# Loading the first layer's convolution image straight from the input, and the first weights in two parts

## The chip, the cores and the metric

The kernel runs on one core of a Trainium2 chip. The metric is the device time of one execution in microseconds (us). Engines are named as the profile names them: PE is TensorE's matmul, PEld its weight load, DVE is VectorE, ACT is ScalarE, POOL is GpSimd, and SP is SyncE, which here only issues DMA transfers. ACT and POOL issue transfers too.

## The reference, cut to what matters

Four layers, each `x = x + layer(group_norm(x))`, on an image of 4 x 32 x 32 x 16 (batch, height, width, channels). Layers 0 to 2 have this form:

```python
first = jnp.einsum('ijpq,bpqc->bijc', M2, inputs)
K = jnp.transpose(G, (2, 3, 4, 0, 1, 5)).reshape(kh, kw, c, h * w * f)
shifted = lax.conv_general_dilated(inputs, K, window_strides=(1, 1), padding='SAME', ...)
shifted = shifted.reshape(b, h, w, h, w, f)
diff = jax.nn.relu(inputs[:, :, :, None, None, :] - shifted)
second = jnp.einsum('ijpq,bpqijc->bijc', W2, diff)
return first - L * second
```

`inputs` is x after a group norm of 8 groups of two channels, with mean and variance over a batch element's whole group. The convolution is 3 x 3 with zero padding and has 16 x 1024 outputs at each of 1024 points; `second` weighs them by W, which has 1024 x 1024 values. Layer 3 is a two-dimensional filter given by a rational transfer function; the change doesn't touch its formulas.

## The kernel before

**The products of a layer.** A layer's 1024 output positions (i, j) are 128 blocks of 8. For a block and a batch element the convolution is a product of nine taps x 16 channels with 128 output columns (8 positions x 16 channels) over 1024 points. The image stands in SBUF with taps and channels on the partitions: three tiles per pair of batch elements, `ims[a]` (a is 0 for batch elements 0 and 1, 1 for 2 and 3). Tiles 0 and 1 hold four taps each, for the upper 16 and the lower 16 image rows in partitions 0 to 63 and 64 to 127; tile 2 holds the ninth tap, split into a rounded part and a remainder. So a product is six matmuls (L357): three tiles by two halves. They accumulate in a PSUM tile of 128 x 1024 (`pt`, four of them in rotation). One DVE instruction (L365) takes the minimum with zero, multiplies by W's rows and sums into `acc`.

**The jobs of `conv_layer`.** Job 0 goes through blocks 0 to 7 with batch elements 0 and 1, job 1 through the same blocks with 2 and 3; then come jobs of eight blocks with all four, and the last eight blocks are again split by pairs. After every product `step()` advances the generators in `todo`, and after every block `beside` goes one step further: `first_term` (the product with M), then, in layer 0, `impulse_response`, which prepares layer 3's filter.

**Weights.** `load_w` brings a tile of W for two blocks (1 MB: 8 rows of 8 KB, each copied to 16 partitions), always on SP's queue, from a pool of six tiles. `load_g` brings eight blocks of G: `ga` (taps of tile 0), `gb` (of tile 1), both into partitions 0 to 63 and again into 64 to 127, and `g9` (the ninth tap, copied eight times). `prepare_g` subtracts the identity's share from `ga` on POOL (L285), casts `g9` on ACT (L289) and takes the remainder on DVE (L292).

**The image of layer 0, as of later layers.** `group_norm` sums on DVE, adds across partitions by small matmuls (L103), subtracts the mean (L119) and makes `rstd` by a square root on ACT and a Newton step on DVE. `store_image` writes the normalised y in three forms into `ys[a]`, a tile with zero borders (memsets L90, L92), copies border rows into `ye[a]` on POOL and ACT, and stores both to a DRAM scratch `img[a]`. `load_image` reads the shifted images back: 24 transfers of 67.5 KB for each pair, in turn on SP, ACT and POOL (L185). In layers 1 and 2 this runs beside the products of the layer before.

**The order at the start.** The order of work is written out by hand; every engine and every queue runs its instructions in the order of the program. Before the first product: load x and the constants, load G's first eight blocks (gb on ACT's queue, the rest on SP's), norm, store both images, `prepare_g`, `load_image(0)`, the first W in two halves, the second W, `load_image(1)`, the third and the fourth W. The rest of W and G follows from within `conv_layer`.

Of the kernel before, what the change touches and what calls it, by code (L numbers as in the profile page):

```python
# [29 lines left out]
F32 = mybir.dt.float32  # L30
F32R = mybir.dt.float32r
AF = mybir.ActivationFunctionType
# [19 lines left out]


@with_exitstack
def conv_stack_kernel(ctx, tc, x, M, W, G, den, num, h0, cst, dft, one, idp, idq, out):
    nc = tc.nc

    const = ctx.enter_context(tc.tile_pool(name="const", bufs=1))
# [18 lines left out]
    ctx.enter_context(tc.manual_schedule())  # L77
    xs = xp.tile([P, B, NBLK], F32, tag="x", name="x")
    nc.sync.dma_start(out=xs, in_=x)
    cs = const.tile([P, 2 * P + C], F32, name="cs")  # L80
    nc.scalar.dma_start(out=cs, in_=cst)
    ident, avg, mid = cs[:, :P], cs[:, P : 2 * P], cs[:, 2 * P :]

# [1 line left out]
    ys, ye, img = [], [], []  # L87
    for a in range(2):
        ys.append(const.tile([P, 3, 2, 4, 34], F32, name=f"y{a}"))
        nc.gpsimd.memset(ys[a], 0.0)  # L90
        ye.append(const.tile([P, 3, 2, 4, 34], F32, name=f"e{a}"))
        nc.gpsimd.memset(ye[a], 0.0)  # L92
        img.append(dram.tile([10, C, 3, ROW], F32, name=f"img{a}"))
    hd = dram.tile([8 + C * HLEN], F32, name="hd")
    fd = dram.tile([P, B, 2, 2, S], F32, name="fd")
# [7 lines left out]
            nc.tensor.matmul(pt[:, h, : s.shape[1]], lhsT=avg[rows], rhs=s[rows], start=True, stop=True)  # L103
        return pt

    def group_norm(xt):


        nb = xt.shape[1]
        vec = lambda name: small.tile([P, B], F32, tag=name, name=name)[:, :nb]  # L110
        s = vec("s")
        nc.vector.tensor_reduce(s, xt, AX.X, ALU.add)  # L112
        yield
        pm = group_sums(s)
        mean = vec("mean")
        nc.vector.tensor_copy(mean, pm[:, 0, :nb])
        nc.vector.tensor_tensor(mean, mean, pm[:, 1, :nb], ALU.add)
        xc = work.tile([P, B, NBLK], F32, tag="xc", name="xc")[:, :nb]
        nc.vector.tensor_tensor(  # L119
            xc, xt, mean.unsqueeze(2).to_broadcast([P, nb, NBLK]), ALU.subtract  # L120
        )
        sq = junkp.tile([P, S * S], F32, tag="junk", name="sq")[:, : nb * NBLK]
        sq = sq.rearrange("p (b n) -> p b n", b=nb)
        nc.vector.tensor_tensor(sq, xc, xc, ALU.mult)
        ss = vec("ss")
        nc.vector.tensor_reduce(ss, sq, AX.X, ALU.add)
        yield
        yield
        pv = group_sums(ss)
        v = vec("v")  # L130
        nc.vector.tensor_scalar(v, pv[:, 0, :nb], 1e-5, None, ALU.add)
        nc.vector.tensor_tensor(v, v, pv[:, 1, :nb], ALU.add)

        r = vec("r")
        nc.scalar.activation(r, v, AF.Sqrt)
        ri = vec("ri")
        nc.vector.reciprocal(ri, r)
        nc.vector.tensor_tensor(ri, ri, v, ALU.mult)
        nc.vector.tensor_tensor(r, r, ri, ALU.add)
        nc.vector.tensor_scalar(r, r, 0.5, None, ALU.mult)  # L140
        rstd = vec("rstd")
        nc.vector.reciprocal(rstd, r)
        return xc, rstd.unsqueeze(2).to_broadcast([P, nb, NBLK])

    ims, yc = {}, {}

    def make_image(a, xt):

# [5 lines left out]
    def store_image(a, xc, rstd):  # L154
        split = lambda t: t.rearrange("p b (cc q) -> p b cc q", q=S)
        whole, hi, lo = (ys[a][:, k, :, :, 1:33] for k in range(3))
        y = work.tile([P, 2, NBLK], F32, tag=f"yc{a}", name=f"yc{a}")
        nc.vector.tensor_tensor(y, xc, rstd, ALU.mult)
        yc[a] = y
        nc.vector.tensor_copy(hi.bitcast(F32R), split(y))  # L160
        nc.scalar.copy(whole, split(y))
        nc.vector.tensor_tensor(lo, split(y), hi, ALU.subtract)  # L162
        nc.gpsimd.tensor_copy(ye[a][96:, :, :, 1:, :], ys[a][96:, :, :, :3, :])  # L163
        nc.scalar.copy(ye[a][:32, :, :, :3, :], ys[a][:32, :, :, 1:, :])
        flat = lambda t: t.rearrange("p k b cc x -> p (k b cc x)")
        rows = img[a].rearrange("p c k x -> p c (k x)")
        nc.sync.dma_start(out=rows[1:9].rearrange("p c x -> (p c) x"), in_=flat(ys[a]))
        nc.scalar.dma_start(out=rows[0], in_=flat(ye[a][7 * C :]))
        nc.scalar.dma_start(out=rows[9], in_=flat(ye[a][:C]))

    def load_image(a):


        ims[a] = [
            imp.tile([P, 4, 2, 4, 34], d, tag=f"im{a}{k}", name=f"im{a}{k}")
            for k, d in enumerate((F32, F32, F32R))
        ]
        taps = [(n // 4, n % 4, 0, TAPS[n]) for n in range(8)]
        taps += [(2, n, 1 + n % 2, 8) for n in range(4)]
        jobs = [(half, *tap) for tap in taps for half in range(2)]  # L180

        jobs.sort(key=lambda job: job[4] // 3 == 2 * job[0])
        for n, (half, k, slot, which, tap) in enumerate(jobs):
            at, p = 64 * half + C * slot, 4 * half + tap // 3
            (nc.sync, nc.scalar, nc.gpsimd)[n % 3].dma_start(  # L185
                out=ims[a][k][at : at + C]
                .bitcast(F32)
                .rearrange("c l b cc x -> c l (b cc x)")[:, :, :RUN],
                in_=img[a][p : p + 4, :, which, tap % 3 : tap % 3 + RUN].rearrange(
                    "l c x -> c l x"  # L190
                ),
            )
# [62 lines left out]
    def chunk(layer, ch):  # L255
        return layer + ch // (NBLK // GC), ch % (NBLK // GC)

    def load_g(layer, ch, other=None):
        layer, ch = at = chunk(layer, ch)
        if layer == 3 or at in gr:  # L260
            return
        ga = gs.tile([P, GC, P], F32, tag="ga", name="ga")
        gb = gs.tile([P, GC, P], F32, tag="gb", name="gb")
        g9 = gp.tile([P, GC, P], F32, tag="g9", name="g9")
        src = G[layer][:, bass.ts(ch, GC * P)]
        for half in range(2):
            rows = slice(64 * half, 64 * half + 64)
            nc.sync.dma_start(out=ga[rows].rearrange("r n m -> r (n m)"), in_=src[:64])
            (other or nc.sync).dma_start(out=gb[rows].rearrange("r n m -> r (n m)"), in_=src[64:P])
        nc.sync.dma_start(  # L270
            out=g9.rearrange("r n m -> r (n m)"),
            in_=src[P : P + C].unsqueeze(0).to_broadcast([8, C, GC * P]),
        )
        gr[at] = ga, gb, g9

    def prepare_g(layer, ch):


        at = chunk(layer, ch)
        if at[0] == 3 or at in gt:  # L280
            return
        ga, gb, g9 = gr[at]

        gv = ga.rearrange("r n (p f) -> r (n p) f", f=C)
        nc.gpsimd.tensor_tensor(  # L285
            gv, gv, mid.unsqueeze(1).to_broadcast([P, GC * 8, C]), ALU.subtract
        )
        gn = gs.tile([P, GC, P], F32R, tag="gn", name="gn")
        nc.scalar.copy(gn, g9)  # L289
        for r in (32, 96):  # L290
            lo = gn[r : r + 32]
            nc.vector.tensor_tensor(lo, g9[r : r + 32], lo.bitcast(F32), ALU.subtract)  # L292
        gt[at] = ga, gb, gn

    wts = []

# [23 lines left out]
        while todo:  # L320
            step()

    def conv_layer(layer, xt, finish, side=()):

        acc = [work.tile([P, 2, NBLK], F32, tag=f"acc{a}", name=f"acc{a}") for a in range(2)]
        xn = xp.tile([P, B, NBLK], F32, tag="x", name="x")
# [11 lines left out]
        for job, (blks, batches) in enumerate(jobs):  # L338
            pairs = job < 2, job >= len(jobs) - 2
            for k, blk in enumerate(blks):  # L340
# [4 lines left out]
                elif k % 2 == 0:  # L345
                    list(load_w())
                if k == (3 if job == 0 else 1):
                    load_g(layer, blk // GC + 1)
                if job and k == 6:
                    prepare_g(layer, blk // GC + 1)  # L350
                wt = wts[64 * layer + blk // 2][:, blk % 2, :]
                for b in batches:
                    pt = pair_psum()
# [32 lines left out]
    def impulse_response():  # L386


        with tc.tile_pool(name="fs", bufs=1) as fs, tc.tile_pool(name="ft", bufs=1) as ft:
# [9 lines left out]
                nc.scalar.dma_start(out=inv[rows], in_=idp)  # L399
            nc.scalar.dma_start(out=ones, in_=one)  # L400
            H = fs.tile([P, len(FCH), 2, 2 * P], F32, name="H")
            yield
            yield
            for ch, (f0, nf) in enumerate(FCH):
                pab = pair_psum()
                for ri in range(2):
# [117 lines left out]
            )  # L524
            yield

    load_g(0, 0, nc.scalar)
    norm = group_norm(xs)
    while True:
        try:  # L530
            next(norm)
        except StopIteration as end:
            xc, rstd = end.value
            break
    store_image(0, xc[:, :2], rstd[:, :2])
    store_image(1, xc[:, 2:], rstd[:, 2:])
    prepare_g(0, 0)
    load_image(0)
    list(load_w(2))
    list(load_w())  # L540
    load_image(1)
    list(load_w())
    list(load_w())
    xs = conv_layer(0, xs, make_image, impulse_response())
    xs = conv_layer(1, xs, make_image)


# [3 lines left out]
    def norm3(a, xt):  # L551
        xc, rstd = yield from group_norm(xt[:, 2 * a : 2 * a + 2])
        nc.vector.tensor_tensor(
            y3[:, :, 31:, 2 * a : 2 * a + 2].rearrange("p cc q b -> p b cc q"),
            xc.rearrange("p b (cc q) -> p b cc q", q=S),
            rstd.rearrange("p b (cc q) -> p b cc q", q=S),
            ALU.mult,
        )

# [77 lines left out]
def _tables():  # L637
# [3 lines left out]
    at = np.arange(P)  # L641
    same = (at[:, None] % C) // 2 == (at[None, :] % C) // 2
    mid = (at % 64 >= 3 * C)[:, None] * np.eye(C)[at % C]
    cst = np.concatenate([np.eye(P), same / (16.0 * NBLK), mid], 1).astype(np.float32)
    at = np.arange(S)
    turn = 2 * np.pi * (np.outer(at, at) % S) / S
    cos, sin = np.cos(turn), np.sin(turn)
# [70 lines left out]
```

## Time and profile before

| | |
|---|---|
| median of three runs | 3175.56 us (3174.41 to 3177.02) |
| profiled execution | 3173.08 us |
| its span, first to last instruction | 3171.3 us |
| PE busy | 3113.8 us, 98% of the span |
| DVE busy | 2059.5 us, 65% |
| ACT, POOL busy | 75.6 us (2%), 233.6 us (7%) |
| mean granted TensorE clock | 0.997 |
| DMA traffic | 322.20 MB, mean 102 GB/s |

The profile shows one execution. Its times count from the first instruction. A timeline row gives the start, the length, engine, line, operation, tile written and tiles read, shapes, and in brackets the idle time of the engine before it with what ended it. A row of stretches gives a stretch's limits and length, each engine's busy time and instructions in it, the granted clock (1.00 is full), the mean busy share of the 16 DMA engines, and GB/s. The chain of waits goes back from the last instruction to what released each step, so it holds what set the end. How the start of the first layer looks:

```profile
0.00:82.90 82.90, 39.91 (x160) 23.57 (x160) 0.94 0.72 138
82.90:114.30 31.40, 31.38 (x160) 19.99 (x162) 1.00 0.56 121
```

These are the matmuls of L357 and their weight loads alone: in the first 82.9 us PE has 39.91 us of them, in the next 31.4 us it has 31.38.

### The profile page before, as it was taken

What the parts mean: (1) busy time and instruction counts of PE and PEld (TensorE: products, weight loads), DVE (VectorE), ACT (ScalarE), POOL (GpSimd) and SP (SyncE); (2) the same over time, 40 slices, a digit from 0 to 9 for tenths busy, and PEclk for the clock granted to TensorE, in tenths of its full rate; (3) what the DMA queues carried; (4) which work ended last, traced back from release to release, by engine and by line L of the source; (5) the groups of instructions that cost most, each with busy time, mean ns of one, the idle gap of its engine ahead of it and who ended that gap; (6) DMA issues with size and microseconds to landing.
All of it is one profiled execution on the core that took longest, in us unless ns stands there. A gap on an engine that the chain in (4) does not pass through costs nothing.

```text
span 3171.3 us, 38906 instructions
## 1 busy us (share of the span) xinstructions
PE 3113.8 (98%) x16068; PEld 1727.0 (54%) x16068; DVE 2059.5 (65%) x3302; ACT 75.6 (2%) x97; POOL 233.6 (7%) x240
## 2 busy tenths in 40 slices
PE   4999999999999999999999999999999999999998
PEld 2544557777777554445555445455445555454454
DVE  3666666666666766666666666676666666666662
ACT  0000000000000000000000000000000000000000
POOL 1002321000000100100000000010010000000000
PEclk9999999999999999999999999999999999999999
DMA  7653344343334564433343334355544444444303
GB/s 139 136 152 96 94 106 112 87 99 95 87 87 105 99 156 115 99 98 87 88 98 96 87 87 102 78 120 149 125 108 102 97 107 106 102 97 106 94 14 54
DMA packets 69549, 322.20 MB, mean 102 GB/s; under 512 B 10570, under 2 KB 19276, under 8 KB 43900
## 3 DMA queue, kind: packets, MB, share of 16 engines
q1 hardware_dynamic: 57448, 300.50, 39.8%
q10 hardware_dynamic: 7620, 11.96, 2.0%
q0 software_dynamic: 4304, 7.26, 1.3%
q8 instruction: 126, 2.06, 0.3%
q14 instruction: 51, 0.42, 0.1%
HBM read 313.01 MB, written 6.67 MB: 101 GB/s over the span
## 4 chain that ended last, share of the span: by engine, by line
PE 96%; DMA 3%; DVE 1%; issue 0%; ACTq 0%; SPq 0%; ACT 0%; POOL 0%; DVEq 0%; POOLq 0%
PE pt L357 94%; DMA w<-in_W_dram 2%; DMA t<-hd 1%; PE pt L218 1%; PE pt L618 1%; DMA im<-img 0%; DVE junk L365 0%; PE pt L103 0%; PE pt L409 0%; PE pt L452 0%; DMA x<-in_x_dram 0%; PE pt L491 0%; DVE s L112 0%; DVE x L380 0%; PE pt L205 0%
## 5 line engine op out<-in xcount | busy, mean ns | idle before, releaser
L365 DVE SCALAR_TENSOR_TENSOR junk<-pt,w 128x1024 f32<-128x1024 f32 x1536 | 1880.6, 1224 | 1033.6 <-PE pt L357 994.2
L357 PE MATMUL pt<-im,ga 64*128 64x512 f32 x6144 | 1684.4, 591 | 29.6 <-issue 18.2
L357 PE MATMUL pt<-im,gb 64*128 64x512 f32 x6144 | 1677.7, 589 | 4.2 <-DMA im<-img 4.2
L357 PE MATMUL pt<-im,gn 64*128 64x512 f32 x3072 | 1349.7, 806 | 0.5 <-DMA im<-img 0.5
L357 PEld LDWEIGHTS pt<-im,gb 64*128 64x128 f32 x6144 | 697.1, 186 | 650.5 <-issue 574.0
L357 PEld LDWEIGHTS pt<-im,ga 64*128 64x128 f32 x6144 | 684.3, 188 | 402.0 <-DVE junk L365 240.1
L357 PEld LDWEIGHTS pt<-im,gn 64*128 64x128 f32 x3072 | 360.0, 186 | 322.5 <-issue 284.5
L285 POOL TENSOR_TENSOR ga<-ga,cs 128x1024 f32<-128x1024 f32 x48 | 113.3, 2361 | 2165.7 <-DMA ga<-in_G_dram 2165.6
L365 DVE DVE_READ_ACCUMULATOR junk<-pt,w 128x1 f32 x1536 | 127.4, 83 | 0.0
L292 DVE TENSOR_TENSOR gn<-g,gn 32x1024 fp32r<-32x1024 f32 x96 | 118.3, 1232 | 9.6 <-ACT gn L289 7.5
L289 ACT CAST gn<-g 128x1024 fp32r<-128x1024 f32 x48 | 50.2, 1047 | 2338.1 <-DMA g<-in_G_dram 2324.3
L618 PE MATMUL pt<-t,y 128*32 128x512 f32 (+4 forms) x448 | 45.3, 436 | 3.4 <-DMA t<-hd 2.6
L242 POOL DMA_DIRECT2D fd<-ft x48 | 25.1, 530 | 224.8 <-DVE ft L235 212.9
L618 PEld LDWEIGHTS pt<-t,y 128*32 128x32 f32 (+1 forms) x448 | 24.0, 123 | 24.7 <-issue 17.6
L593 DVE TENSOR_TENSOR xo<-xo,pt 32x512 f32<-32x512 f32 x5 | 3.4, 682 | 37.7 <-PE pt L618 37.6
L185 POOL DMA_DIRECT2D im<-img x48 | 24.5, 516 | 12.4 <-DMA img<-y 8.8
L218 PE MATMUL pt<-mt,yt 128*64 128x512 f32 x96 | 21.9, 599 | 0.0
L218 PEld LDWEIGHTS pt<-mt,yt 128*64 128x64 f32 x96 | 6.4, 136 | 13.7 <-issue 9.4
L163 POOL COPY e<-y 32x612 f32<-32x612 f32 x6 | 4.2, 697 | 129.3 <-DVE y L162 127.9
L430 POOL TENSOR_TENSOR H<-H,d 128x256 f32<-128x256 f32 (+1 forms) x10 | 8.2, 824 | 66.7 <-DVE d L435 66.3
L103 PE MATMUL pt<-s,cs 64*128 64x2 f32 (+1 forms) x28 | 2.9, 266 | 9.3 <-DVE s L112 9.3
L430 POOL TENSOR_TENSOR t<-s 128x256 f32<-128x256 f32 (+1 forms) x15 | 11.3, 753 | 0.0
(68 smaller groups left out, 162.4 us busy)
## 6 DMA issues: line engine op xcount, KB each, us to landing
w<-in_W_dram SPq DMA_DIRECT2D x191, 1024.0 KB
ga<-in_G_dram SPq DMA_DIRECT2D x96, 256.0 KB
g<-in_G_dram SPq DMA_DIRECT2D x48, 512.0 KB
gb<-in_G_dram SPq DMA_DIRECT2D x94, 256.0 KB
mt<-in_M_dram SPq DMA_DIRECT2D x24, 512.0 KB
t<-hd ACTq DMA_DIRECT2D x32, 160.0 KB
t<-hd SPq DMA_DIRECT2D x32, 160.0 KB
im<-img SPq DMA_DIRECT2D x48, 67.5 KB
```

The costliest lines, as they stand in the source:

```text
L163: nc.gpsimd.tensor_copy(ye[a][96:, :, :, 1:, :], ys[a][96:, :, :, :3, :])
L185: (nc.sync, nc.scalar, nc.gpsimd)[n % 3].dma_start(out=ims[a][k][at : at + C] .bitcast(F32) .rearrange("c l b cc x -> c l (b cc x)")[:, :, ...
L218: nc.tensor.matmul(pf[64 * h : 64 * h + 64], lhsT=yt[:, 4 * part + k].rearrange("k b c -> k (b c)"), rhs=mts[k][:, h, :], start=(k == 0), ...
L242: nc.gpsimd.dma_start(out=fv[h, cc, b], in_=ft[at : at + C, cc])
L285: nc.gpsimd.tensor_tensor(gv, gv, mid.unsqueeze(1).to_broadcast([P, GC * 8, C]), ALU.subtract)
L289: nc.scalar.copy(gn, g9)
L292: nc.vector.tensor_tensor(lo, g9[r : r + 32], lo.bitcast(F32), ALU.subtract)
L357: nc.tensor.matmul(pt[:, half, :], lhsT=w[rows, blk % GC, :], rhs=im[rows, :, b % 2, :, :S], start=n == 0, stop=n == 2,)
L365: nc.vector.scalar_tensor_tensor(junk, pt.rearrange("p h m -> p (h m)"), 0.0, wt, ALU.min, ALU.mult, accum_out=acc[b // 2][:, b % 2, blk : ...
L430: mul = lambda o, u, w: nc.gpsimd.tensor_tensor(o, u, w, ALU.mult)
L593: nc.vector.tensor_tensor(out, out, src, ALU.add)
L618: nc.tensor.matmul(bank[cols].rearrange("n (j r) -> n j r", j=C)[:, :, 8 * cc :], lhsT=y3[:, cc, at : at + width, :].rearrange("p q b -> p ...
```

## The change

For layer 0 alone, the image isn't made from y by way of DRAM any more. The host program lays a copy of x out in the taps' arrangement, shifted and with zeros around it, as a new input `raw` (128 partitions x 2 pairs x 3 tiles x 1088 values; 3.3 MB). Six transfers of 557 KB bring it into `ims[a][0]`, `ims[a][1]` and a new tile `nine[a]`. There it is normalised: ACT adds minus the mean to each tile and batch element, POOL sets to zero again what lies outside of the image, and DVE and ACT multiply by `rstd`; the ninth tap's rounded part and remainder are made on DVE from `nine` with two new columns of the constants, `is_lo` and `sign`. The group norm runs for each pair alone, the second pair's as a generator that `conv_layer` takes up at block 5 of job 0, so its steps stand between the products. The first eight blocks of G come in two parts, two blocks and six, with gb and g9 on ACT's queue, and `prepare_g` takes them in two parts as well; the second part's ACT and DVE steps stand after the first product.

The new order on SP's queue is: x, tiles 0 and 1 of the first pair, ga's first part, the first W in two halves, ga's second part, W 2, 3 and 4, the three tiles of the second pair, and then the next eight blocks of G. ACT's queue has the constants, a square root on a dummy tile (which loads its function table), `nine` of the first pair, gb and g9 of both parts, and then ACT's own work. The memsets of `ys` and `ye` move into `impulse_response`, one with each of four steps where two empty ones were. The layers after layer 0 load their images as before.

```diff
+    def load_first(a, which):
+
+        if a not in ims:
+            image_tiles(a)
+            nine[a] = st.tile([P, 4, 2, 4, 34], F32, name=f"nine{a}")
+        eng = nc.scalar if (a, which) == (0, 2) else nc.sync
+        eng.dma_start(
+            out=(nine[a] if which == 2 else ims[a][which]).rearrange("p l b cc x -> p (l b cc x)"),
+            in_=raw[:, a, which],
+        )
+
+    def first_image(a, xt):
+
+        im0, im4, im8 = ims[a]
+        each = [(t, b) for t in (im0, im4, nine[a]) for b in range(2)]
+        of = lambda t, b: t[:, :, b].rearrange("p l cc x -> p l (cc x)")
+
+        def outside(t, rows, l, cc, x):
+            nc.gpsimd.memset(t[rows, l, :, cc, x], 0.0)
+
+        def center(mean):
+            neg = small.tile([P, 2], F32, tag="neg", name="neg")
+            nc.vector.tensor_scalar(neg, mean, -1.0, None, ALU.mult)
+            for t, b in each:
+                v = of(t, b)
+                nc.scalar.activation(v, v, AF.Identity, bias=neg[:, b : b + 1])
...
+            for g in range(0, P, 32):
+                outside(im0, slice(g, g + 16), *left)
...
+        xc, rstd = yield from group_norm(xt[:, 2 * a : 2 * a + 2], center)
+        rlo = small.tile([P, 2], F32, tag="rlo", name="rlo")
+        for b in range(2):
+            v0, v4, v8, v = (of(t, b) for t in (im0, im4, im8, nine[a]))
+            r = rstd[:, b : b + 1]
+            nc.vector.tensor_scalar(v0, v0, r, None, ALU.mult)
+            nc.scalar.activation(v4, v4, AF.Copy, scale=r)
+            if b == 0:
+                nc.vector.tensor_scalar(rlo, rstd, is_lo, None, ALU.mult)
+            nc.vector.tensor_scalar(v8, v, r, None, ALU.mult)
+            nc.scalar.activation(v, v, AF.Copy, scale=rlo[:, b : b + 1])
+            nc.vector.scalar_tensor_tensor(v8, v8.bitcast(F32), sign, v, ALU.mult, ALU.add)
+            yield
+        normalise(a, xc, rstd)
+        yield
...
+    def load_g(layer, ch, other=None, parts=(slice(0, GC),)):
...
+        other = other or nc.sync
+        flat = lambda t: t.rearrange("r n m -> r (n m)")
+        for part in parts:
+            src = G[layer][:, (ch * GC + part.start) * P : (ch * GC + part.stop) * P]
+            for half in range(2):
+                rows = slice(64 * half, 64 * half + 64)
+                nc.sync.dma_start(out=flat(ga[rows, part]), in_=src[:64])
+                other.dma_start(out=flat(gb[rows, part]), in_=src[64:P])
+            other.dma_start(
+                out=flat(g9[:, part]),
+                in_=src[P : P + C].unsqueeze(0).to_broadcast([8, C, (part.stop - part.start) * P]),
+            )
+            yield
...
+                if pair and job == 0 and k == 5:
+                    todo.append(pair)
...
-            yield
-            yield
+            for t in ys + ye:
+                nc.gpsimd.memset(t, 0.0)
+                yield
...
-    load_g(0, 0, nc.scalar)
-    norm = group_norm(xs)
...
-    store_image(0, xc[:, :2], rstd[:, :2])
-    store_image(1, xc[:, 2:], rstd[:, 2:])
-    prepare_g(0, 0)
-    load_image(0)
-    list(load_w(2))
-    list(load_w())
-    load_image(1)
-    list(load_w())
-    list(load_w())
-    xs = conv_layer(0, xs, make_image, impulse_response())
...
+    table = small.tile([P, 2], F32, tag="neg", name="table")
+    nc.gpsimd.memset(table, 1.0)
+    nc.scalar.activation(table, table, AF.Sqrt)
+    nine = {}
+    with tc.tile_pool(name="st", bufs=1) as st:
+        halves = slice(0, 2), slice(2, GC)
+        loads = load_g(0, 0, nc.scalar, halves)
+        for which in range(3):
+            load_first(0, which)
+        next(loads)
+        list(load_w(2))
+        list(loads)
+        for _ in range(3):
+            list(load_w())
+        for which in range(3):
+            load_first(1, which)
+        image = first_image(0, xs)
+        for _ in range(3):
+            next(image)
+        first, second = (prepare_g(0, 0, part) for part in halves)
+        next(first)
+        next(image)
+        list(first)
+        list(image)
+        todo.append(second)
+        xs = conv_layer(0, xs, make_image, impulse_response(), first_image(1, xs))
```

## The prediction, made before the changed kernel was run

> **What bounds the kernel now.** I read the page first, then the chain of waits in order of time, then the start as a timeline and in stretches. The page's row of engines and the chain's shares say that TensorE is the bound:
>
> ```profile
> PE 3113.8 (98%) x16068; PEld 1727.0 (54%) x16068; DVE 2059.5 (65%) x3302; ACT 75.6 (2%) x97; POOL 233.6 (7%) x240
> PE 96%; DMA 3%; DVE 1%; issue 0%; ACTq 0%; SPq 0%; ACT 0%; POOL 0%; DVEq 0%; POOLq 0%
> ```
>
> Only the 3% that is DMA can be won here. The chain in order of time puts most of it ahead of 82.92 us:
>
> ```profile
> 15.38 3.73 DMA im<-img
> 19.13 5.61 DMA im<-img
> 24.75 28.65 DMA w<-in_W_dram
> 53.42 2.42 DMA im<-img
> 56.52 24.59 DMA w<-in_W_dram
> 81.64 1.24 DVE junk L365 x2
> 82.92 47.45 PE pt L357 x216
> ```
>
> The columns are start, length and what held the end. Image loads (L185) come first, then loads of W. From 82.92 us TensorE runs without a stop. What is done by then? The first job is eight blocks by two batches, 16 products of six matmuls, each consumed by one L365. The thirteenth L365 frees one of four PSUM tiles and lets product 17 start:
>
> ```profile
> 53.52 1.23 DVE L365 SCALAR_TENSOR_TENSOR junk<-pt,w 128x1024 f32<-128x1024 f32 x1 [6.21 <-DMA w<-in_W_dram]
> 71.95 1.23 DVE L365 SCALAR_TENSOR_TENSOR junk<-pt,w 128x1024 f32<-128x1024 f32 x1 [13.18 <-DMA w<-in_W_dram]
> 81.64 1.22 DVE L365 SCALAR_TENSOR_TENSOR junk<-pt,w 128x1024 f32<-128x1024 f32 x1 [4.44 <-DMA w<-in_W_dram]
> 82.92 1.20 PE L357 MATMUL pt<-im,ga 64*128 64x512 f32 x4
> 84.67 2.37 POOL L285 TENSOR_TENSOR ga<-ga,cs 128x1024 f32<-128x1024 f32 x1 [55.73 <-DMA ga<-in_G_dram]
> ```
>
> So the change is worth 82.92 minus the time at which product 17 starts afterwards, and a faster first image alone is worth nothing: products 5, 9 and 13 wait for the second, third and fourth W. What limits W is seen in stretches (the last two numbers are the DMA share and GB/s):
>
> ```profile
> 2.00:4.00 2.00, 0.00 (x0) 0.00 (x0) 0.00 (x0) 1.28 (x1) 1.66 (x3) 1.00 1.01 304
> 20.00:41.00 21.00, 9.33 (x20) 4.82 (x20) 1.23 (x2) 0.00 (x0) 5.35 (x11) 1.00 0.88 136
> 60.00:67.00 7.00, 2.94 (x16) 1.15 (x12) 0.00 (x0) 0.00 (x0) 0.00 (x0) 0.92 1.05 136
> 68.00:79.00 11.00, 5.76 (x22) 2.80 (x24) 4.93 (x8) 0.00 (x0) 0.00 (x0) 0.63 0.49 109
> 80.00:88.00 8.00, 7.88 (x42) 4.54 (x40) 5.95 (x9) 0.00 (x0) 2.37 (x1) 1.00 0.52 116
> ```
>
> Alone (68 to 79) W keeps only half of the DMA engines busy and moves 109 GB/s. The loads of ga and gb, issued behind it at 57 to 59.6 us, run beside it at 60 to 67 (share 1.05) and go on at 80 to 88, share 0.52, once W is done; the subtraction on ga (L285) waited till 84.67. I read this as half of such a load on W's eight engines, queued behind W, and half on the other eight. g9 reads its rows through the same leading 8 as W, so I put it wholly on W's half. That half, "W's half" below, is the bound of the start.
>
> In sentences apart: the Trainium skill ("DMA: Bandwidth & Descriptors", "Rules for kernel authors") says the same of W, a leading broadcast of 8 copies confines the transfer to at most 8 engines. Its "Specifications" give some 27 GiB/s an engine, 232 GB/s for eight (an estimate from that page), by which the 5.24 MB below would take 23 us and not 45.5. The stretch shows 109 GB/s, so I go by the row.
>
> **What is removed.** For layer 0 the two stores of y, four of e, 48 image loads, four memsets and the copies behind them. The memsets (four of 0.78) return in `impulse_response`, on a GpSimd busy for 46 of 130 us at 290 to 420; if that were not free, 3.1 us late for a side chain that nothing awaits before layer 3. Two yields more there shift that chain by two blocks, about 16 us, with hundreds spare (its last matmuls are at 535, the layer ends past 1,000).
>
> **The first image afterwards.** x lands at 4.2 as now. ScalarE's queue holds nine0, the gb and g9 loads of both parts, and only then the six centring activations; the rest of gb waits for nine0, so I have them start at 10.3. An activation with a bias, 128x256, takes 0.469 us (L418), a cast of 1024 1.047 (L289): 0.71 for 544 elements, six 4.3. Sqrt is queued behind them (14.8), five small DVE steps 1.0, four DVE passes of 544 (0.42 for 256, 0.69 for 512, so 0.72; 2.3 with rlo), the G remainder 0.7: the first product ends near 20, now 38.2. GpSimd's 13 border memsets (0.1 to 0.2 each, by 128x1 at 0.10) lie beside this. The second W lands near 39, worked out as below from 3.2 MB, so this chain may slip ten us before it counts.
>
> **What then decides: W's half of the queue.** The last raw piece of images 2 and 3 (nine1) is queued on SP behind all four W. Bytes on W's half ahead of its end:
> - x, constants, three raw pieces: (0.26 + 0.14 + 3 x 0.557) / 2 = 1.04 MB; rate 304 / 2 = 152 GB/s (2 to 4 us): 6.8 us.
> - four W 4.19, g9 0.52, half of ga and gb 0.52: 5.24 MB at 115 (80 to 88 and 68 to 79): 45.5.
> - W slowed by traffic on the other half: W 3 and 4 now took 24.6 us for 2.10 MB, less 18.2 at 115 and 2.1 for starting and landing: 4.3 lost beside 0.52 MB of G, 8.2 us per MB. Afterwards about 0.72 MB of G runs so: 5.9. For 0.84 MB of raw rows there is no row: 0 to 6.9; I take 1.0, since contiguous rows of x ran fast.
> - three raw pieces, 0.84 MB at 152: 5.5 (4.3 at 195 per half, the rate of the image stores at 14.8 to 15.6, 396 GB/s in all; 12.3 at 68, half of the 136 of 20 to 41).
> - first issue and start 1.5, landing 1.2.
>
> Sum 67.4 us. No SP wait adds to it: each waits for a load that stands earlier in the same queues.
>
> **The second image's chain** starts there, its steps standing in DVE's order before the L365 of products 15 and 16, which so wait too, but they would wait for W 4 anyway. Two centrings 1.3 to 1.4, Sqrt 0.2, five steps 1.0, v0 0.7: product 17 can start 3.3 after nine1, its last matmuls at 5.0; L365 of product 15 (1.3) stands before the second batch, three passes 2.2, so product 18 ends at 9.0. Two products take 3.9 (1.963 each), so it is as if product 17 had started at 5.1. TensorE has idled since about 60 and is cold, as at 73.24, where four matmuls took 2.08 instead of 1.02: 1.0 more. 67.4 + 6.1 = 73.5.
>
> **Behind it** nothing new: the next G and fifth W land at 67.4 + 4.6 + 4.6 + 9.1 = 86 and are needed at 73.5 + 31.4 = 105.
>
> Sum: 73.5 - 82.9 = -9.4 us. The profiled execution took 3173.08 (span 3171.3), so 3163.7; the median of the runs is 3175.56, 2.5 above it, so 3166.
>
> **Rivals.**
> - *No collisions* (chance 0.2): raw rows at the stores' 195 and nothing lost on W: 67.4 - 5.9 - 1.0 - 1.5 - 1.2 = 57.8, product 17 at 64, 3157. For it: x's 304 GB/s. Against: 136 GB/s at 60 to 67.
> - *The expected gain stays in the queue* (0.17): by 81.1 now W's half carried 4.19 of W, 1.04 of G, 0.2 of x and constants and half of 1.0 stored and 3.3 loaded for the images, some 7.6 MB, 94 GB/s over all; at that rate the 7.1 MB still ahead of nine1 land at 77, product 17 at 83: 3175, no change. Against: W stood still between 51.5 and 57 now, which the new order avoids.
> - *Slower* (0.08): the raw rows, 26 KB apart, collide with W as the old image loads did at 20 to 41. At 68 GB/s per half they cost 27.6 and not 12.3 us, and their other half costs W the full 6.9: nine1 at 88.6, product 17 at 94.7, 3187. It decides once nine1 lands after 77.
> - That the change doesn't do what it says, I exclude: the removed stores are not in the changed queues.
>
> **Numbers.** The forecast has 0.55: 3166, its own range 3160 to 3172. With the rivals, 3154 to 3177. About 0.2% (6.4 us) is what a measurement can tell from no change: faster 0.69, same 0.22, slower 0.09.
>
> **What would show it.** Right: the first product near 20; DVE idle on W before products 5, 9 and 13 as now; TensorE without a stop from 70 to 77, released by the second image's chain, not by W; DMA share near 0.5 at 110 GB/s for most of the start. Wrong: another wait after 100 us, a raw load far from 150 GB/s per half, or a first image so late that products 1 to 4 hold W's buffers.

## The result, and the profile after

The kernel after takes 3161.23 us (median of four runs, 3159.61 to 3162.89). The kernel before, run beside it, takes 3175.19 (3174.41 to 3177.02). The ratio is 0.9955, 95% interval 0.9938 to 0.9972: 14.0 us faster, where 9.4 were forecast. The profiled execution has a span of 3157.7 us, 13.6 less than before.

On the page, the row of engines and the chain's shares:

```profile
PE 3114.3 (99%) x16076; PEld 1548.8 (49%) x16076; DVE 2072.4 (66%) x3329; ACT 87.5 (3%) x116; POOL 228.9 (7%) x250
PE 97%; DMA 2%; DVE 1%; issue 0%; SPq 0%; ACT 0%; ACTq 0%; DVEq 0%
```

TensorE has the same 3114 us of work and the same bound. What the chain had as DMA has gone from 3% to 2% of the span, in whole per cents. The chain in order of time (start, length, what held the end) shows where:

```profile
1.69 6.95 DMA gb<-in_G_dram
...
10.94 27.71 DMA w<-in_W_dram
...
38.78 1.24 DVE junk L438 x2
...
40.06 9.81 PE pt L430 x40
...
56.55 4.04 PE pt L430 x18
60.59 6.73 issue
67.33 49.73 PE pt L430 x240
```

The image loads are gone from it. The reduction is now L438 and the product L430. A wait for W still stands there (10.94 to 38.65), and the unbroken run of TensorE starts at 67.33 instead of 82.92. What it waits for just before is under the name "issue", which means that the profile found no releaser. The timeline gives it:

```profile
38.78 1.22 DVE L438 SCALAR_TENSOR_TENSOR junk<-pt,w 128x1024 f32<-128x1024 f32 x1 [6.50 <-DMA w<-in_W_dram]
47.22 1.23 DVE L438 SCALAR_TENSOR_TENSOR junk<-pt,w 128x1024 f32<-128x1024 f32 x1 [3.20 <-DMA w<-in_W_dram]
56.17 1.23 DVE L438 SCALAR_TENSOR_TENSOR junk<-pt,w 128x1024 f32<-128x1024 f32 x1 [1.45 <-DMA w<-in_W_dram]
62.25 1.39 ACT L182 ACTIVATE nine<-nine,neg 128x544 f32<-128x544 f32 x2 [2.13 <-DMA nine<-in_raw_dram]
64.58 2.34 POOL L356 TENSOR_TENSOR ga<-ga,cs 128x1024 f32<-128x1024 f32 x1 [0.47 <-POOL nine L175]
64.81 2.41 DVE L202 TENSOR_SCALAR im<-im,rstd 128x544 f32<-128x544 f32 x1
67.33 2.08 PE L430 MATMUL pt<-im,ga 64*128 64x512 f32 x4 [6.75 <-issue]
70.48 0.50 DVE L202 TENSOR_SCALAR im<-im,rstd 128x544 f32<-128x544 f32 x1
```

The first three rows are the reductions of products 5, 9 and 13, each waiting for its W (53.52, 71.95 and 81.64 before). The fourth is the arrival of nine1, at 62.25. The sixth is the multiplication of the second image's first tile by `rstd`; it ends at 67.22, and product 17 starts at 67.33. Set it beside the last row, the same instruction for the next batch element: 0.50 us there, 2.41 here, where it runs beside GpSimd's subtraction (64.58 to 66.92) and ends 0.3 behind it.

In stretches (the last three numbers are granted clock, DMA share and GB/s):

```profile
31.00:36.00 5.00, 5.00 (x28) 2.51 (x26) 1.23 (x2) 0.00 (x0) 0.00 (x0) 1.00 1.04 154
39.00:47.00 8.00, 6.93 (x26) 3.40 (x28) 4.71 (x8) 0.00 (x0) 0.00 (x0) 0.79 0.59 140
68.00:75.00 7.00, 7.00 (x28) 3.17 (x26) 5.48 (x10) 2.93 (x4) 0.00 (x0) 0.70 0.51 208
```

and for the products' matmuls alone, up to product 17:

```profile
0.00:67.30 67.30, 36.70 (x160) 17.85 (x161) 0.96 0.69 168
```

PE now has 36.7 of 67.3 us before product 17, where it had 39.9 of 82.9.

To compare kernels to better than a run's scatter, one instant serves: the start of the 48th reduction, in the third job. What TensorE still stops for behind it costs the kernels nearly the same: in between the distance to the kernel before shifts by up to 3.1 us for a time, but at the last reduction (the 1536th) it is again what it was at the 48th, within 0.7 us, in every kernel below. The last 60 us, layer 3, vary by up to 5 us from one execution to the next. Before:

```profile
146.90 1.22 DVE L365 SCALAR_TENSOR_TENSOR junk<-pt,w 128x1024 f32<-128x1024 f32 x1 [0.73 <-PE pt L357]
```

and after:

```profile
133.57 1.23 DVE L438 SCALAR_TENSOR_TENSOR junk<-pt,w 128x1024 f32<-128x1024 f32 x1 [0.73 <-PE pt L430]
```

So the whole gain, 13.3 us, is made before 134 us. It is called "the gain at the 48th reduction" below.

### The profile page after: what moved, and what is told of

Read it like the earlier page. It is cut to its first block, busy times and chain, and to the rows that moved or that the text cites. A ratio compares the mean times of both kernels' runs of the same rounds, so it can differ in the third digit from the quotient of the medians.

```text
span 3157.7 us, 38913 instructions
## 1 busy us (share of the span) xinstructions
PE 3114.3 (99%) x16076; PEld 1548.8 (49%) x16076; DVE 2072.4 (66%) x3329; ACT 87.5 (3%) x116; POOL 228.9 (7%) x250
## 4 chain that ended last, share of the span: by engine, by line
PE 97%; DMA 2%; DVE 1%; issue 0%; SPq 0%; ACT 0%; ACTq 0%; DVEq 0%
PE pt L430 95%; DMA w<-in_W_dram 1%; PE pt L701 1%; PE pt L282 1%; DMA t<-hd 1%; DVE junk L438 0%; DMA gb<-in_G_dram 0%; PE pt L483 0%; PE pt L102 0%; PE pt L526 0%; PE pt L565 0%; DVE s L111 0%; DVE x L453 0%; PE pt L269 0%; SPq L336 0%
## 5 line engine op out<-in xcount | busy, mean ns | idle before, releaser
L438 DVE SCALAR_TENSOR_TENSOR junk<-pt,w 128x1024 f32<-128x1024 f32 x1536 | 1880.9, 1225 | 997.0 <-PE pt L430 969.7
L430 PE MATMUL pt<-im,ga 64*128 64x512 f32 x6144 | 1588.2, 591 | 20.8 <-DVE im L202 8.7
L430 PE MATMUL pt<-im,gb 64*128 64x512 f32 x6144 | 1579.3, 589 | 0.0
L430 PE MATMUL pt<-im,gn 64*128 64x512 f32 x3072 | 1253.6, 806 | 0.0
L430 PEld LDWEIGHTS pt<-im,gb 64*128 64x128 f32 x6144 | 598.8, 186 | 723.6 <-issue 722.6
L430 PEld LDWEIGHTS pt<-im,ga 64*128 64x128 f32 x6144 | 602.3, 188 | 454.6 <-DVE junk L438 281.8
L430 PEld LDWEIGHTS pt<-im,gn 64*128 64x128 f32 x3072 | 300.9, 186 | 360.0 <-issue 358.4
L356 POOL TENSOR_TENSOR ga<-ga,cs 128x1024 f32<-128x1024 f32 (+2 forms) x49 | 113.9, 2325 | 2126.3 <-DMA ga<-in_G_dram 2125.8
L438 DVE DVE_READ_ACCUMULATOR junk<-pt,w 128x1 f32 x1536 | 127.9, 83 | 0.0
L363 DVE TENSOR_TENSOR gn<-g,gn 32x1024 fp32r<-32x1024 f32 (+2 forms) x98 | 121.9, 1244 | 5.8 <-ACT gn L360 3.7
L360 ACT CAST gn<-g 128x1024 fp32r<-128x1024 f32 (+2 forms) x49 | 50.4, 1028 | 2313.9 <-DMA g<-in_G_dram 2185.0
L249 POOL DMA_DIRECT2D im<-img x32 | 16.2, 515 | 9.1 <-DMA img<-y 8.8
```

What stands on the lines that cost most here:

```text
L249: (nc.sync, nc.scalar, nc.gpsimd)[n % 3].dma_start(out=ims[a][k][at : at + C] .bitcast(F32) .rearrange("c l b cc x -> c l (b cc x)")[:, :, ...
L356: nc.gpsimd.tensor_tensor(gv, gv, mid.unsqueeze(1).to_broadcast([P, gv.shape[1], C]), ALU.subtract)
L430: nc.tensor.matmul(pt[:, half, :], lhsT=w[rows, blk % GC, :], rhs=im[rows, :, b % 2, :, :S], start=n == 0, stop=n == 2,)
L438: nc.vector.scalar_tensor_tensor(junk, pt.rearrange("p h m -> p (h m)"), 0.0, wt, ALU.min, ALU.mult, accum_out=acc[b // 2][:, b % 2, blk : ...
```

## The experiments

My theory was that the second image's chain sets the end, that it hangs on what is queued ahead of nine1 behind W, and that the first image has slack. The rivals were that the first image's speed makes the gain, or that G's two parts do, or that W's eight engines aren't what holds the queue.

### The order alone, with the old image

The kernel before, with nothing changed but that the second image's loads are issued behind W 3 and 4:

```diff
-    load_image(1)
     list(load_w())
     list(load_w())
+    load_image(1)
```

> The kernel before, with its third and fourth W queued ahead of the second pair's image loads; nothing else changed. Theory (what sets the start of the steady products is the last landing on W's half of the DMA engines): SP no longer stands still for the image loads between 51.5 and 57 us, so W 4 lands some 6 to 9 us earlier; the second pair's loads end after it and give part of that back. Product 17 starts at 75 to 79 us instead of 82.9, time 3168 to 3172. Rival (the gain of the change is that the first image is ready earlier): nothing is gained, product 17 at 82.9, 3175.

Measured: 3166.8 us (3164.19 to 3171.32), ratio 0.998 (0.9968 to 0.9991). The 48th reduction starts at 140.27, 6.6 us earlier. Its chain in order of time, in part:

```profile
23.78 13.49 DMA im<-img
...
37.29 33.97 DMA w<-in_W_dram
...
72.09 2.37 DMA im<-img
74.46 0.14 issue
74.60 25.58 PE pt L357 x108
```

The first product is as late as before, and product 17 starts at 74.60 instead of 82.92. Both figures are a little better than I expected (75 to 79, and 3168 to 3172). Half of the change's 13.3 us is thus to be had by putting W ahead of the second image; a faster first image isn't needed for it.

### The first image eight us later

The kernel after, with six copies of a 128 x 1024 tile on ScalarE ahead of the first centring. They compute nothing that is used.

```diff
+            if a == 0:
+                spin = st.tile([P, 1024], F32, name="spin")
+                nc.gpsimd.memset(spin, 0.0)
+                for _ in range(6):
+                    nc.scalar.copy(spin, spin)
```

> The changed kernel, with six copies of a 128x1024 tile onto itself on ScalarE ahead of the first pair's centring, 6.3 us that compute nothing used. Theory: the first image may slip by six us for nothing, since products 5, 9 and 13 still wait for W: first product 6 us later, third and fourth W and the 48th reduction within 1 us of the changed kernel's (133.6). Rival (the first image is what sets the gain): the 48th reduction moves by the 6.3 us, to 140, and so does the time.

Measured: 3162.9 us, ratio 0.9962 (0.9947 to 0.9977). The first reduction is 8.0 us late:

```profile
30.06 1.22 DVE L443 SCALAR_TENSOR_TENSOR junk<-pt,w 128x1024 f32<-128x1024 f32 x1
```

The 48th starts at 132.59, not later but 1.0 earlier. That isn't the delay's doing: in this execution the second W landed 1.1 earlier (the fifth reduction starts at 37.72 instead of 38.78), and all that follows moved with it. So eight us of the first image are worth nothing on their own, and the rival falls that far; the change brought the first reduction forward by 16.2 us in all (38.26 to 22.03).

### G in one part

```diff
-        halves = slice(0, 2), slice(2, GC)
+        halves = (slice(0, GC),)
...
```

> The changed kernel, with the first eight blocks of G loaded and prepared in one part again (two parts undone; the rest of the change kept). Theory: the parts only let the first products start earlier, and these wait for W afterwards; W's half carries the same bytes, so the 48th reduction, at 133.6 us in the changed kernel, starts within 1.5 us of that; the time is the changed kernel's. Rival (the early start of the first products is part of the gain): the first product ends some 8 us later and the 48th reduction 3 us or more later.

Measured: 3161.98 us, ratio 0.9959 (0.9943 to 0.9974). The first reduction comes at 24.77, only 2.7 us later and not the eight that I expected, and the 48th at 133.78, 0.2 later. The two parts add nothing to the time.

### What stands ahead of nine1

First, the second image's raw rows ahead of W 4, with the norm still taken up at block 5 of job 0:

```diff
-        for _ in range(3):
+        for _ in range(2):
             list(load_w())
         for which in range(3):
             load_first(1, which)
+        list(load_w())
```

> The changed kernel, with the second pair's three raw pieces queued ahead of W 4 instead of behind it. Theory: W's half carries the same bytes, so W 4 lands at 61 to 63 us, where nine1 landed; and as the second image's chain stands in VectorE's order behind products 13 and 14, which wait for W 4, it still ends 5 to 7 us after that: product 17 at 66 to 69, no change within 2 us. Rival (it is the landing of the second image that holds product 17): it lands 9 us earlier and product 17 starts at 60 to 63.

Measured: 3160.41 us, ratio 0.9956 (0.994 to 0.9971); 48th reduction at 133.76. The image is there early, but the last steps of its norm stand behind reductions 13 and 14 in VectorE's order, and the 13th now waits for W until 61.14:

```profile
61.14 1.23 DVE L438 SCALAR_TENSOR_TENSOR junk<-pt,w 128x1024 f32<-128x1024 f32 x1 [4.75 <-DMA w<-in_W_dram]
65.30 2.35 DVE L202 TENSOR_SCALAR im<-im,rstd 128x544 f32<-128x544 f32 x1
```

No change, as expected. Then the norm at block 3 as well:

```diff
-                if pair and job == 0 and k == 5:
+                if pair and job == 0 and k == 3:
```

> As the run with the raw pieces ahead of W 4, and the second image's chain taken up at block 3 instead of block 5 of job 0. Theory: the chain now stands ahead of products 11 and 12 in VectorE's order, ends near 58, hidden behind W 4's landing at 61 to 63; product 17 then needs only product 13's reduction and starts at 62.5 to 65, 3 to 5 us earlier than in the changed kernel. Rival (the place in VectorE's order doesn't matter): product 17 starts where it does in the run with the raw pieces ahead of W 4 alone.

Measured: 3157.74 us, ratio 0.9949 (0.9926 to 0.9971). TensorE runs without a stop from 62.82, with product 16; the 48th reduction starts at 129.09, 4.5 us earlier than in the kernel after. The second image's steps now stand before reductions 11 and 12 (57.91 and 61.54) and cover the wait for W 4; reduction 13 at 63.02 waits for nothing:

```profile
62.82 1.53 PE L430 MATMUL pt<-im,ga 64*128 64x512 f32 x4 [0.42 <-DVE junk L438]
63.02 1.22 DVE L438 SCALAR_TENSOR_TENSOR junk<-pt,w 128x1024 f32<-128x1024 f32 x1
```

Block 3 with the raw rows still behind W 4 wasn't run, so the pair of edits is shown and not each alone. What stood ahead of nine1 in the queue and in VectorE's order thus did set the end.

### VectorE beside GpSimd

The subtraction on `ga` of the second eight blocks is held back until the second image's ninth-tap tile is done, by a copy of two of its columns on GpSimd:

```diff
+        if at == (0, 1):
+            hold = small.tile([P, 2], F32, tag="neg", name="hold")
+            nc.gpsimd.tensor_copy(hold, ims[1][2][:, 0, 1, 0, :2].bitcast(F32))
```

> The changed kernel, with GpSimd's subtraction on the second eight blocks of G held back until the second pair's image is done (a tiny copy from that image stands before it). Theory: the first multiplication of the second image by rstd on VectorE took 2.41 us instead of 0.50 because GpSimd's subtraction ran beside it; held back, it takes 0.5, product 17 starts 1.9 us earlier, near 65.4, and the time falls by 1.9. Rival: the long instruction waited for something else (a late memset, a transfer): it stays at 2.4 us and product 17 at 67.3.

Measured: 3161.63 us, ratio 0.9966 (0.9947 to 0.9986); 48th reduction at 130.12, 3.45 us earlier. The fifth reduction, nine1's arrival, and the same row of VectorE's as above:

```profile
37.58 1.23 DVE L441 SCALAR_TENSOR_TENSOR junk<-pt,w 128x1024 f32<-128x1024 f32 x1 [5.85 <-DMA w<-in_W_dram]
60.93 1.39 ACT L182 ACTIVATE nine<-nine,neg 128x544 f32<-128x544 f32 x2 [0.74 <-DMA nine<-in_raw_dram]
63.50 0.50 DVE L202 TENSOR_SCALAR im<-im,rstd 128x544 f32<-128x544 f32 x1
```

0.50 instead of 2.41, so the 1.9 us are GpSimd's. Another 1.3 us are nine1's, at 60.93 instead of 62.25. They are already there at the second W, whose reduction starts at 37.58 instead of 38.78, long before the hold acts; so they belong to this execution and not to the edit. Of the 3.45 us only some 2 are therefore the hold's. The median shows none of it. In the two profiled executions the last reduction starts 3.4 us earlier, and what follows it takes 63.4 us instead of 60.5, so there layer 3's scatter hides the gain; for the other runs this wasn't seen.

### W on all sixteen engines

W's rows are 8 with 16 copies each. Here the first four tiles of W are read from an input in which these rows stand written out for 128 partitions; the tiles hold the same values. It makes the program's input 4.2 MB larger.

```diff
+            part = src[:, bass.ts(k, n)].unsqueeze(1).to_broadcast([8, C, n])
+            if len(wts) <= 4:
+                part = wide[len(wts) - 1][:, bass.ts(k, n)]
...
+    first = arrays["W0"][0, :, :8].reshape(8, 4, 2 * S * S).transpose(1, 0, 2)
+    arrays["wide"] = np.repeat(first, C, axis=1)
```

> The changed kernel, with the first four W tiles read from a copy that the host lays out in 128 rows (each row of W sixteen times, 4.2 MB, the same bytes into the same tiles), so that the transfer's outer dimension is 128 and not 8. Theory (W's eight engines at 115 to 130 GB/s are what bounds the start): the four W tiles run on all 16 engines, near 350 GB/s, and all have landed by 35 us; no reduction waits for W any more, TensorE runs nearly without a stop from the first product on, product 17 starts at 50 to 54 us, and the 48th reduction at 114 to 120 instead of 133.6; time 3143 to 3149. Rival (the total rate of DMA is the bound at the start, not the engines that W uses): W lands less than 5 us earlier and the time falls by less than 5.

Measured: 3146.7 us (3145.04 to 3147.17), ratio 0.9913 (0.9896 to 0.9929). The 48th reduction starts at 118.57, 15.0 us earlier than in the kernel after, and product 17 at 52.55. A stretch of it:

```profile
16.00:30.00 14.00, 13.12 (x58) 6.45 (x60) 10.85 (x19) 3.62 (x6) 1.81 (x1) 1.00 1.02 312
```

All engines are busy at 312 GB/s, where the kernel after had 140 and 154 in the two stretches shown above from before 47 us. VectorE waits for no W any more. That W, as it was read, bounds the start is shown by this; the rival, that the amount of bytes or the total rate of DMA bounds it, falls. Which property of W's loads it was isn't: the edit lets W use all engines, and it also ends the reading of each row sixteen times. The number of engines can't be all of it, for the kernel after had all engines busy from 31 to 36 us too (share 1.04) and moved 154 GB/s, half as much.

Product 17 has some 2.1 us of GpSimd in it here as well: the subtraction, from 48.88, meets a VectorE instruction of two columns, which took 0.16 elsewhere:

```profile
48.97 2.27 DVE L139 TENSOR_TENSOR ri<-ri,v 128x2 f32<-128x2 f32 x1
51.28 0.16 DVE L140 TENSOR_TENSOR r<-r,ri 128x2 f32<-128x2 f32 x1
```

With the two edits on nine1's place and the hold on GpSimd added:

> As the run with the wide W, and with the raw pieces of the second pair ahead of W 4, its chain taken up at block 3 of job 0, and GpSimd's next subtraction held back behind it. Theory: what is left at the start is TensorE's own work from the first product near 20 us, 16 products of 1.963 us and one wait for G's second part: product 17 at 49 to 52, without a stop and warm, the 48th reduction at 113 to 116, 2 to 5 us before the run with the wide W alone; time 3140 to 3145. Rival: the chain in VectorE's order now delays the reductions instead, and nothing is gained on that run.

Measured: 3145.75 us, ratio 0.9911 (0.9896 to 0.9926); 48th reduction at 116.87, 1.7 us earlier than with the wide W alone and 0.9 later than the 116 that I expected at the latest; the time, too, is just above what I expected. The hold released the subtraction too early: it now ran beside the next VectorE step, which took 1.85 us. The times of the two kernels can't be told apart.

### The price of G beside W

The next eight blocks of G are issued later, on ScalarE's queue at the first block of job 1, so that nothing runs beside W 3 and 4 or the raw rows but what belongs to them:

```diff
-                nc.sync.dma_start(out=flat(ga[rows, part]), in_=src[:64])
+                (other if at == (0, 1) else nc.sync).dma_start(out=flat(ga[rows, part]), in_=src[:64])
...
-                if k == (3 if job == 0 else 1):
+                if layer == 0 and job < 2:
+                    if job == 1 and k == 0:
+                        list(load_g(0, 1, nc.scalar))
+                elif k == (3 if job == 0 else 1):
```

> The changed kernel, with the second eight blocks of G issued only after the second image is done (on ScalarE's queue, ahead of block 0 of job 1), so that none of it runs beside the W tiles of job 0. This measures the loss that the prediction priced at 8.2 us per MB of G beside W. If the price held: 0.52 MB less, W 4's reduction and the second pair's last centring (56.2 and 62.3 us in the changed kernel) come 4.3 us earlier, near 52 and 58. If it was set too high, as the landings of W after the change suggest (8.4 and 9.0 us apart, with half of that G between them): 1 to 2.5 us earlier, 54 to 55 and 60 to 61. In both cases the multiplication by rstd takes 0.5 us again, as GpSimd's subtraction comes later.

Measured: 3156.96 us (two runs), ratio 0.9946 (0.9926 to 0.9965). Reductions 5, 9 and 13 start at 37.58, 46.21 and 55.00, the last 1.2 us earlier than in the kernel after. From the timeline, the fifth reduction, nine1's arrival, and what became late instead:

```profile
37.58 1.22 DVE L441 SCALAR_TENSOR_TENSOR junk<-pt,w 128x1024 f32<-128x1024 f32 x1 [5.49 <-DMA w<-in_W_dram]
59.31 1.39 ACT L182 ACTIVATE nine<-nine,neg 128x544 f32<-128x544 f32 x2 [1.00 <-DMA nine<-in_raw_dram]
94.05 1.05 ACT L360 CAST gn<-g 128x1024 fp32r<-128x1024 f32 x1 [26.66 <-DMA g<-in_G_dram]
98.94 1.54 PE L433 MATMUL pt<-im,ga 64*128 64x512 f32 x4 [2.68 <-issue]
```

nine1 is 2.9 us earlier and job 1 about 5, but job 2 then waits for G, and the 48th reduction starts at 133.11, 0.5 earlier than in the kernel after. By the price that I had put on such traffic, 8.2 us per MB, W 4 should have come 4.3 us earlier. Reductions 5 and 9 are 1.2 and 1.0 earlier; the 13th waits for its product and not for W any more, so W 4 was there by 55.00 or a little before. From W 2 to W 3 it is 8.6 us, with G beside them it was 8.4.

Not all of nine1's 2.9 us is G's. The second W comes at 37.58 in the run with the hold as well, where G is still beside it, so the first 1.2 belong to the execution. From the second W to nine1 it takes 59.31 - 37.58 = 21.7 us here. With G in its place it took 23.5 in the kernel after and 23.35 in the runs with the hold (60.93 - 37.58) and with the late first image (61.07 - 37.72). G's price in this stretch is thus 1.6 to 1.7 us, below the 4.3 and within the 1 to 2.5 of the expectation.

### All together

The wide W, nine1's two edits, the hold placed one step later, and `gb` and `g9` of G's second part on SP's queue behind the first W, since ScalarE's first centring stood behind their issue:

```diff
-                other.dma_start(out=flat(gb[rows, part]), in_=src[64:P])
+                (other if part.start == 0 else nc.sync).dma_start(out=flat(gb[rows, part]), in_=src[64:P])
...
+            nc.gpsimd.tensor_copy(hold, yc[1][:, 0, :2])
```

> As the run with the wide W, the raw pieces ahead of W 4 and the chain at block 3, with two changes: the second part of gb and g9 is issued on SP behind the first W instead of on ScalarE ahead of the centring, and GpSimd's held-back subtraction waits for the second pair's last normalising (yc) and not for its image alone. Theory: the centring starts when the first raw piece has landed, near 7 us and not 10, and ends near 11.5; the first product starts 2 to 2.5 us earlier, near 14; yc takes 0.42 again instead of 1.85. The 48th reduction starts at 112 to 114.5 instead of 116.9, the time falls by 2.5 to 4.5 us against that run, to 3141 to 3144. Rival: G's second part lands later on SP's queue and products 5 on wait for it by as much as was won: 116 to 118.

Measured: 3140.94 us (3139.31 to 3144.28), ratio 0.9896 (0.988 to 0.9913); 48th reduction at 113.97. From its timeline, the first centring and the first product:

```profile
6.76 1.39 ACT L182 ACTIVATE im<-im,neg 128x544 f32<-128x544 f32 x2 [4.06 <-DVE ss L127]
14.07 2.08 PE L433 MATMUL pt<-im,ga 64*128 64x512 f32 x4 [6.66 <-DVE im L202]
```

Centring starts at 6.76 instead of 10.01, and the 48th reduction gains 2.9 us on the run with the wide W and the hold. Both edits are in this: the first reduction starts 2.2 us earlier (20.70 against 22.93) and the ninth 2.0, and the VectorE step that took 1.85 takes 0.42 again. What each would give alone wasn't run; but with W out of the way a first image that is two us earlier does reach the ninth reduction, where eight us reached nothing before. This version beats both: it is 33.6 us under the kernel before, where the kernel after is 14.0 under it. Of the 19.6 us between the two (133.57 - 113.97), 15.0 come from W's layout, which the change didn't touch.

## Why the prediction was right, and where its sizes were off

**The first image.** The first centring starts at 10.01 (10.3 forecast), Sqrt at 13.86 (14.8), and the first product ends near 20.4 (20). That it "may slip ten us before it counts" was right as far as it was tried: eight us cost nothing.

**The second W** landed at 38.78 (near 39); so close a hit is in part luck, for it was 37.58 and 37.72 in two other executions with the same queue ahead of it. W's outer dimension is eight rows, each read sixteen times, and not the eight copies that the prediction names; only g9's is. For the half of the engines this makes no difference, as the share of 0.49 for W alone shows. That VectorE would wait for W before products 5, 9 and 13, and that TensorE would then run on from the second image's chain and not from W, was right.

**nine1** came at 62.25, not 67.4. Here a term was mis-sized. From the second W to nine1 the forecast had 67.4 - 39 = 28.4 us; it took 23.5, so nearly the whole miss lies there. In that 28.4 stood 18.2 for two tiles of W, 5.5 for the raw pieces, and the rest, 4.7, for "W slowed by traffic on the other half". With the next eight blocks of G moved away, the same stretch takes 21.7, so G's price in it is at most 1.7 us, not 4.7, and the queue by itself needs 21.7, not 23.7. The collisions were priced too high (8.2 us per MB), and 115 GB/s was a little low. I had drawn the price from W 3 and 4 of the kernel before, 4.3 us longer than at 115 GB/s, and blamed G for all of it. What else delayed them there wasn't tried.

**The chain behind nine1** was forecast at 6.1 us effective and took 7.3, counted back from the 48th reduction (82.92 - 13.33 = 69.59, less 62.25). Product 17 itself started 5.1 us after nine1 instead of 3.3. The forecast gave VectorE's `v0` 0.7 us and hadn't looked at what GpSimd does at that moment. It took 2.41, and holding GpSimd back gave the 1.9 us back. The cold clock was right: the first four matmuls took 2.08, and the granted clock was 0.50 from 67 to 72 us.

**The sum.** 5.1 us too long at nine1 and 1.2 too short behind it leave 3.9, and so does the 48th reduction: 13.3 gained for 9.4 forecast. That the two errors pull opposite ways is luck. The mechanism was right: W's loads, then the second image's chain, and no credit for the first image. Nothing new appeared behind 100 us, as forecast. The last 0.7 between 13.3 and the medians' 14.0 lies within what layer 3 varies by.

**The rivals.** "No collisions" had nine1 at 57.8 and product 17 at 64; the kernel lies about midway between it and the forecast: G beside W costs less than was forecast, but not nothing. "The gain stays in the queue" and "slower" needed nine1 past 77; nine1 came 6.1 us behind W 4, so the three raw pieces, 0.84 MB on W's half, had 137 GB/s and not 68. Of what was to show the steps right, two did not come. TensorE's run without a stop was to start between 70 and 77 us and started at 67.33, for the reasons above. And the DMA share was to be near 0.5 at 110 GB/s for most of the start; it was 1.04 at 31 to 36 us and 0.69 over all, with more on the other eight engines than I had thought. W as the bound stands nevertheless, since another layout of it took the next 15 us away; that the eight engines are the reason, and not the repeated reading of its rows, stays argued.

**What the gain is made of.** 6.6 of the 13.3 us are to be had by the order alone, with the old image. The other 6.7 come with the image straight from the input; whether from fewer bytes, from no passage through DRAM or from the shorter chain wasn't separated.

## What to carry to other kernels

Ask first which event lets the bounding engine run without a stop, then what lies ahead of it on its queue, by the half of the engines that each load uses; a load that comes earlier elsewhere is worth nothing. A price for two loads that collide should come from the same load with and without the other beside it, in more than one execution, and not from one slow stretch. Where a chain of small steps is exposed, look at what every other engine does in those few us, also an engine that shares no data with it.

## What was not expected of the hardware

**VectorE beside GpSimd.** The 128 x 544 multiplication (L202) takes 0.50 us alone and 2.41, 2.35 and 2.41 when it starts beside GpSimd's 2.3 us subtraction (kernel after, raw rows ahead of W 4, G in one part), ending 0.3 us behind it. With GpSimd held back it took 0.50 again. It isn't a matter of size: with the wide W an instruction on two columns (L139) took 2.27 instead of 0.16. And it doesn't strike every instruction: of the 1536 reductions of the kernel after none took more than 1.227 us, though subtractions of 2.3 us ran beside some of them. The Trainium skill ("GPSIMD Engine Reference", "1. Specifications") says that GpSimd shares its SBUF interfaces with VectorE, and that they contend where VectorE runs in a two-port mode or has two SBUF inputs. That agrees with L139, which has two inputs in SBUF, and with the reductions, which have one there and one in PSUM. It agrees with the multiplication if that ran in such a mode; no run here shows its mode.

**W's rate isn't one number.** The same load on half of the engines moved at 117 to 125 GB/s for W 3 and 4 (a tile of 1.05 MB in 8.4 to 9.0 us), but the stretch at 68 to 75 us above shows 208 GB/s at a share of 0.51 with nothing but W under way, where W alone had 109 at 0.49 in the kernel before (68 to 79 us). What sets it wasn't found.
